# Layer 1 of a four-layer megakernel: the turning of a row's probabilities moved one row of scores later, and layer 2's layernorm rows turned in other banks

## The chip, the cores and the metric

The kernel runs on one core of a Trainium2 chip. It is one program of some 40,500 instructions that computes four transformer-like layers in one launch. The metric is the device time of one execution in microseconds (us). The kernel before takes 2910.99 us, the median of three runs (2909.49 to 2912.12).

The engines are named as in the profile: PE is TensorE, PEld its weight loads, DVE is VectorE, ACT is ScalarE, POOL is GpSimd, SP is SyncE, which issues DMAs.

## The reference

The input is x of 4 sequences with 512 tokens of width 256, in float32. Each of the four layers does

```
xn = layernorm(x)
x  = x + attention_i(xn) + ffn_i(xn)
```

with another kind of attention and feed-forward in each. The change touches layer 1's attention, and the layernorm that ends layer 1. Layer 1's attention has 16 heads, and keys and values that come from one compressed vector of 64 per token:

```
q     = rmsnorm(x @ wq_a) @ wq_b          -> 16 heads of 128 (plain) + 64 (rotary)
ckv   = x @ wkv_a                         -> 64 (compressed) + 64 (rotary, one for all heads)
kv    = rmsnorm(ckv[:64]) @ wkv_b         -> 16 heads of 128 (keys) + 128 (values)
probs = softmax(causal(q @ k.T * 192**-0.5))
x    += (probs @ v) @ wo
```

Layer 1's feed-forward is the sum of a gated unit of width 1024 and of a product-key memory: each token picks 8 of 512 experts, whose rows are gathered from HBM.

## The kernel before, in words

Everything is in tiles of 128 partitions. x stays in SBUF as 16 tiles of 128 tokens; `xnT` holds the layernormed x with the width on the partitions. Matrix products are float32, so that one product of the program is two passes on PE; a turn (transpose) of a 128x128 block is a product with the identity in one pass.

PSUM has eight banks, which `Ctx.ps` (L49) gives out under three tags: four "mm", two "tr" and two "acc". A bank is given out again once its last reader is done.

Layer 1's attention is `latent_pieces` (L1071). The heads' key and value weights are folded into the queries and the output weights (`carry`, L1095, once for each group of four heads), so that scores are taken against the compressed vector and its rotary part, `kf`, 128 rows in all, and the probabilities multiply the compressed values `cv`. After the projections, one loop (L1293) goes over 64 rows of scores: for each group of four heads, each sequence, each pair of heads, and each head of the pair. A row `s` is one head of one sequence, 512 queries by 512 keys, in four steps i = 0 to 3:

- `probabilities(s, i)` (L1153) calls `exp_scores` (L1035): PE takes the scores of query tile i against the first (i + 1) x 128 keys into an "mm" bank (L1042); DVE adds the mask, takes the extreme of each query and writes to SBUF (L1045); ACT takes the exponential and its sum (L1049). At i = 2 the sums of tiles 0 to 2, and at i = 3 that of tile 3, are inverted on DVE (L1165), and ACT scales the tiles by them (L1167).
- `turned(s - 1, i)` (L1169) turns, for the row before, the blocks of key tile j = i: 4 - j blocks (L1174) into a "tr" bank. The bank is copied to `PT` by DVE for j = 0 and 2 and by ACT for j = 1 and 3 (L1178); the copy is issued after the next step's turns.
- At i = 0 of odd rows the rotary part of the next queries is combined (`rotate`, L1146), and at i = 0 of even rows the next pair's queries are computed (`queries`, L1120, four wide products, copied out by ACT at L1137 to L1142).
- At the end of each even row, with both heads of the pair before turned, the product of values and probabilities (L1328, 16 narrow products in an "acc" bank) is taken; ACT copies it to `zT` (L1334), and `out_pieces` (L1275) multiplies it by the output weights (L1282) in pieces that later steps place between their own work.

These pieces are generators. `weave` (L566) draws from several of them by planned costs (each `yield` states one): the attention, the product-key memory (`product_key_pieces`, L1341, with gathers on POOL at L1435 and much work on DVE), the gated unit (`glu_pieces`, L224), and near the end the routing of layer 2's first half. The recording order is then not the final order: a scheduler places each engine's instructions by priority (the recording order) and by when it takes their inputs and banks to be ready, so that the order on each engine is its own. After that each engine runs its list strictly in order and waits on semaphores.

When all three contributions to a sequence of x are in, `layernorms` (L124) is called for it (L2339): DVE computes the statistics and the rows (L149), and after eight more steps PE turns them by 128x128 blocks, four to a bank, two banks to a sequence (L159), and ACT copies each bank into `xnT` (L164). The bank's tag is "mm" where `apart` is set and "tr" elsewhere.

## Time and profile before

| what | us |
|---|---|
| median of three runs | 2910.99 |
| the profiled execution, its own time | 2915.69 |
| its span, first to last instruction | 2913.9 |
| PE busy in the span | 2860.2 (98%) |
| PEld busy | 1920.8 (66%) |
| DVE busy | 2131.7 (73%) |
| ACT busy | 1401.9 (48%) |
| POOL busy | 862.4 (30%) |
| turns of probabilities in layer 1 (L1174) | 640 blocks, 857.2 to 1456.7 |
| mean granted TensorE clock | 0.996 |

The page's span is that of the profiled execution, which is an ordinary one with its own time; durations and waits come from it. A busy PE is drawn with modelled ends: products overlap in the pipeline, so that a product of 512 columns is drawn 0.59 long while the next may start 0.43 after it. A wait in the lists is the drawn idle time of an engine before an instruction, put down to what released it last. The granted clock is the share of full speed that TensorE ran at.

### The profile page before, as it was taken

What the parts mean: (1) busy time and instruction counts of PE and PEld (TensorE: products, weight loads), DVE (VectorE), ACT (ScalarE), POOL (GpSimd) and SP (SyncE); (2) the same over time, 40 slices, a digit from 0 to 9 for tenths busy, and PEclk for the clock granted to TensorE, in tenths of its full rate; (3) what the DMA queues carried; (4) which work ended last, traced back from release to release, by engine and by line L of the source; (5) the groups of instructions that cost most, each with busy time, mean ns of one, the idle gap of its engine ahead of it and who ended that gap; (6) DMA issues with size and microseconds to landing.
All of it is one profiled execution on the core that took longest, in us unless ns stands there. A gap on an engine that the chain in (4) does not pass through costs nothing.

```text
span 2913.9 us, 40511 instructions
## 1 busy us (share of the span) xinstructions
PE 2860.2 (98%) x13767; PEld 1920.8 (66%) x13767; DVE 2131.7 (73%) x5421; ACT 1401.9 (48%) x3354; POOL 862.4 (30%) x687
## 2 busy tenths in 40 slices
PE   9999999999999999999999999999999999999999
PEld 5566665666655655555577688888888756666666
DVE  6778778787778787888775687777777666666666
ACT  4444445454366666667733554444444333333332
POOL 0565655656510033333035100000000043333331
PEclk9999999999999999999999999999999999999999
DMA  2433333333320144444234544444444300000000
GB/s 106 119 109 115 113 98 95 109 116 97 109 82 17 54 101 124 116 107 112 79 120 120 164 118 125 144 130 130 147 124 141 102 1 22 22 22 22 22 1 30
DMA packets 138687, 268.60 MB, mean 92 GB/s; under 512 B 19729, under 2 KB 99105, under 8 KB 134129
## 3 DMA queue, kind: packets, MB, share of 16 engines
q1 hardware_dynamic: 124016, 218.20, 24.4%
q0 software_dynamic: 14176, 47.04, 6.5%
q8 instruction: 109, 1.79, 0.3%
q14 instruction: 98, 0.79, 0.1%
q10 hardware_dynamic: 288, 0.79, 0.1%
HBM read 202.25 MB, written 54.26 MB: 88 GB/s over the span
## 4 chain that ended last, share of the span: by engine, by line
PE 59%; DVE 7%; ACT 4%; DMA 2%; issue 1%; SPq 0%; POOL 0%; DVEq 0%; ACTq 0%
PE mm L358 17%; PE acc L358 7%; PE mm L1042 6%; PE tr L358 6%; PE acc L1709 5%; PE acc L1058 4%; PE mm L177 3%; PE acc L266 1%; PE acc L1328 1%; DVE pr L1045 1%; PE tr L1174 1%; ACT pr L1049 1%; PE mm L185 1%; PE mm L2121 1%; ACT pr L1167 1%
## 5 line engine op out<-in xcount | busy, mean ns | idle before, releaser
L1049 ACT ACTIVATE pr<-pr,nm 128x128 f32<-128x128 f32 (+3 forms) x512 | 286.4, 560 | 297.6 <-DVE nm L1045 293.4
L1045 DVE CUSTOM_DVE_ANT_0 pr<-mm,late 128x128 f32<-128x128 f32 (+3 forms) x512 | 246.0, 483 | 115.9 <-PE mm L1042 114.3
L177 PE MATMUL mm<-xnT,wu 128*128 128x512 f32 x624 | 283.2, 595 | 0.9 <-DVE cy L620 0.5
L369 ACT COPY part<-mm 128x512 f32<-128x512 f32 (+1 forms) x372 | 177.9, 479 | 210.8 <-PE mm L358 202.6
L358 PE MATMUL mm<-token_sums,unit_sums 128*128 128x512 f32 (+1 forms) x624 | 268.1, 512 | 3.6 <-ACT part L369 3.6
L1435 POOL DMA_INDIRECT e<-in_p_experts,ids x128 | 127.7, 998 | 463.7 <-DVE x L206 358.3
L177 PE MATMUL mm<-xnT,w_in 128*128 128x512 f32 x512 | 230.9, 594 | 2.8 <-DVE cy L620 2.8
L520 DVE SCALAR_TENSOR_TENSOR x<-acc,cw,x 128x128 f32<-128x128 f32 x372 | 128.7, 346 | 106.8 <-PE acc L358 105.1
L177 PEld LDWEIGHTS mm<-xnT,wu 128*128 128x128 f32 x624 | 115.4, 190 | 126.6 <-issue 117.9
L620 DVE SCALAR_TENSOR_TENSOR cy<-mm,ws,cy 128x509 f32<-128x509 f32 (+2 forms) x216 | 159.8, 744 | 40.9 <-ACT cy L616 37.1
L1042 PE MATMUL mm<-kf,qf 128*128 128x128 f32 (+3 forms) x512 | 180.2, 443 | 3.8 <-DVE nm L1045 1.9
L785 ACT ACTIVATE xD<-xc,ws 128x128 f32<-128x128 f32 x256 | 83.6, 390 | 193.3 <-POOL y L826 182.8
L802 POOL TENSOR_TENSOR G<-G,CB 128x1024 f32<-128x1024 f32 x64 | 151.1, 2361 | 76.8 <-DVE G L765 76.8
L1042 PE MATMUL mm<-k,q 128*128 128x128 f32 (+3 forms) x512 | 170.5, 438 | 2.6 <-DVE nm L1045 2.3
L358 PEld LDWEIGHTS acc<-down_sums,hidden_sums 128*128 128x128 f32 x744 | 111.7, 191 | 85.1 <-issue 83.4
L177 PEld LDWEIGHTS mm<-xnT,w_in 128*128 128x128 f32 x512 | 95.8, 190 | 107.2 <-issue 91.8
L1709 PEld LDWEIGHTS acc<-PT,V 128*128 128x128 f32 x1280 | 153.8, 193 | 5.1 <-issue 1.7
L1709 PE MATMUL acc<-PT,V 128*128 128x128 f32 x1280 | 153.9, 276 | 0.0
L302 POOL TENSOR_TENSOR down_sums<-wu 128x256 f32<-128x256 f32 x8 | 5.8, 730 | 498.4 <-DMA wu<-in_o_units 498.4
L765 DVE TENSOR_TENSOR_SCAN G<-G,eye 128x1024 f32<-128x1024 f32 x64 | 147.2, 2300 | 0.1
L1174 PEld LDWEIGHTS tr<-con,pr 128*128 128x128 f32 x640 | 82.3, 141 | 89.9 <-ACT pr L1167 26.7
L503 DVE TENSOR_TENSOR whole<-mm,part 128x512 f32<-128x512 f32 x128 | 88.5, 692 | 68.9 <-PE mm L358 68.9
(456 smaller groups left out, 6735.1 us busy)
## 6 DMA issues: line engine op xcount, KB each, us to landing
turned<-Y SPq DMA_DIRECT2D x252, 160.0 KB, 2.6
PT<-turned SPq DMA_DIRECT2D x63, 640.0 KB, 3.9
G<-own SPq DMA_DIRECT2D x64, 512.0 KB, 4.7
w_in<-in_m_units SPq DMA_DIRECT2D x16, 1024.0 KB, 5.9
eb<-since SPq DMA_DIRECT2D x96, 128.0 KB, 3.5
wu<-in_o_units SPq DMA_DIRECT2D x6, 1536.0 KB, 6.6
wo<-in_m_units SPq DMA_DIRECT2D x16, 512.0 KB, 4.3
psw<-pes SPq DMA_DIRECT2D x128, 64.0 KB, 2.0
```

Source lines behind the costliest of these rows:

```text
L177: c.nc.tensor.matmul(out, lhsT=w[:, d, cols], rhs=c.xnT[:, d, tokens], start=(d == 0), stop=(d == 1))
L358: self.kept(self.c.nc.tensor.matmul(bank, lhsT=lhsT, rhs=rhs, start=first, stop=True, skip_group_check=not first))
L369: self.c.nc.scalar.copy(r, bank)
L520: c.nc.vector.scalar_tensor_tensor(x, bank, self.factor(u, tt), x, ALU.mult, ALU.add)
L620: nc.vector.scalar_tensor_tensor(y[:, j:], src[:, : SEQ - j], conv[:, k, 3 - j : 4 - j], y[:, j:], ALU.mult, ALU.add,)
L765: tc.keep_in_program_order(nc.vector.tensor_tensor_scan(flat, flat, eye.rearrange("p h t -> p (h t)"), 0.0, ALU.mult, ALU.add))
L802: nc.gpsimd.tensor_mul(G, G, seqs[b][2][:, t, :][:, None, :].to_broadcast([P, HG, P]))
L1042: kept(nc.tensor.matmul(sc, lhsT=q[:, i * P : n], rhs=k[:, :n], start=True, stop=True))
L1045: nc.vector.tensor_tensor_reduce(out=pr, in0=sc, in1=late[:, SEQ - n :], scale=scale, scalar=-NEG, op0=ALU.add, op1=ALU.min, accum_out=nm,)
L1049: nc.scalar.activation(pr, pr, AF.Exp, bias=nm, scale=-1.0, accum_out=total)
L1435: nc.gpsimd.indirect_dma_start(out=e, out_offset=None, in_=a["p_experts"], in_offset=bass.IndirectOffsetOnAxis(ap=ids[:, t, k : k + 1], ax ...
L1709: kept(nc.tensor.matmul(zs[:, i], lhsT=head["V"][:, j, h, :], rhs=head["PT"][:, :, i * (i + 1) // 2 + j, :], start=(j == 0), stop=(j == i),))
```

## The change

Two edits. In the loop of layer 1 the four steps of 64 rows become one counter n, with s, i = divmod(n, 4); `turned` is called for step n - 5 instead of n - 4, which is one step of scores later, and the values' product follows the last turn of its pair, so that it too stands one step later, after the first step of the next row of scores. The placing of `rotate`, of `queries`, and of the pieces stays by i and s. The second edit gives `layernorm` and `layernorms` an argument `bank`, and the call for the layernorm after layer 1 passes "mm". From L1291 on, lines of the changed kernel have a number lower by one, and from L2339 on higher by one.

```
-def layernorms(c, seqs, lag, tokens=None, stats=None, apart=False):
+def layernorms(c, seqs, lag, tokens=None, stats=None, apart=False, bank="tr"):
...
-            pt = c.ps("mm" if apart else "tr")
+            pt = c.ps("mm" if apart else bank)
...
-    for s in range(65):
+    for n in range(4 * 65 + 1):
+        s, i = divmod(n, TPB)
         if s < 64:
-            prs[s] = []
-        for i in range(TPB):
-            if s < 64:
-                probabilities(s, i)
-            if s > 0:
-                if i == 0:
-                    PTs[s - 1] = c.tile(pool, [P, 1280], "PT")
-                ready, copy = copy, turned(s - 1, i)
-                if ready:
-                    ready()
-            if i == 0 and s % 2 == 1 and s < 63:
-                rotate(*turning)
-            yield 0.85
-            if i % 2:
-                yield from islice(pieces, 1)
-            if i == 0 and s % 2 == 0 and s < 62:
-                turning = queries(s // 2 + 1)
-                yield 2.6
-        if copy:
-            copy()
-            copy = None
-        if s > 0:
-            del prs[s - 1]
-        if s % 2 == 1:
-            continue
-        if s == 0:
+            if i == 0:
+                prs[s] = []
+            probabilities(s, i)
+        done, j = divmod(n - TPB - 1, TPB)
+        if done >= 0:
+            if j == 0:
+                PTs[done] = c.tile(pool, [P, 1280], "PT")
+            ready, copy = copy, turned(done, j)
+            if ready:
+                ready()
+        if i == 0 and s % 2 == 1 and s < 63:
+            rotate(*turning)
+        yield 0.85
+        if i % 2:
+            yield from islice(pieces, 1)
+        if i == 0 and s % 2 == 0 and s < 62:
+            turning = queries(s // 2 + 1)
+            yield 2.6
+        if done < 0 or j < TPB - 1:
+            continue
+        copy()
+        copy = None
+        del prs[done]
+        if done % 2 == 0:
             continue
...
-        p = s // 2 - 1
+        p = done // 2
...
-                    rhs=PTs[s - 2 + h][:, START[j] : START[j] + SEQ - j * P],
+                    rhs=PTs[done - 1 + h][:, START[j] : START[j] + SEQ - j * P],
...
-        c.parts(3, lambda b: layernorm(c, b, halves[b // 2][b % 2 * SEQ : (b % 2 + 1) * SEQ, :]))
+        c.parts(3, lambda b: layernorm(
+            c, b, halves[b // 2][b % 2 * SEQ : (b % 2 + 1) * SEQ, :], bank="mm"
+        ))
```

More of the change, by code (lines that the diff above doesn't have):

```diff
@@ L116, in rsqrt, with layernorm @@
     c.nc.vector.reciprocal(out, s)
-def layernorm(c, b, tokens=None, apart=False):
-    layernorms(c, [b], 8, tokens, apart=apart)
-def layernorms(c, seqs, lag, tokens=None, stats=None, apart=False):
+def layernorm(c, b, tokens=None, apart=False, bank="tr"):
+    layernorms(c, [b], 8, tokens, apart=apart, bank=bank)
+def layernorms(c, seqs, lag, tokens=None, stats=None, apart=False, bank="tr"):
     nc, pool = c.nc, c.ln
```

## The prediction

> **What bounds the kernel now.** I read the busy time by stage first, then who waits on TensorE in the stage that the change touches, then single waits in the timeline. The stage of layer 1's rows of scores runs from 857 to 1462 us. Columns: stretch, its length, busy time and instructions of PE, PEld, DVE, ACT and POOL, granted clock, DMA share, GB/s.

> ```profile
> 0.00:857.00 857.00, 842.42 (x3939) 521.20 (x3939) 658.48 (x987) 397.84 (x858) 440.41 (x299) 1.00 0.35 106
> 857.00:1462.00 605.00, 587.77 (x2728) 343.69 (x2728) 486.96 (x1694) 411.25 (x1091) 120.81 (x122) 0.99 0.33 88
> 1462.00:2914.00 1452.00, 1429.96 (x7103) 1055.94 (x7101) 986.23 (x2742) 592.83 (x1406) 301.17 (x266) 1.00 0.29 86
> ```

> TensorE is the bound in all three, and in the stage it is drawn idle for 605.0 - 587.8 = 17.2 us, the most per microsecond of the three. Only time that TensorE loses there can come back. The same stage's waits (us in total, times, longest), first of the matmuls, then of the weight loads:

> ```profile
> PE tr L1174 <- ACT pr L1167: 5.3, 14, 1.5
> PE tr L1174 <- ACT PT L1178: 3.5, 4, 1.4
> PE mm L1042 <- DVE nm L1045: 1.9, 2, 1.1
> PE tr L1174 <- DVE PT L1178: 1.4, 5, 0.5
> PE tr L159 <- ACT PT L1178: 1.2, 1, 1.2
> ```
> ```profile
> PEld tr L1174 <- ACT pr L1167: 26.7, 67, 2.0
> ...
> PEld tr L1174 <- ACT PT L1178: 12.6, 20, 2.0
> PEld tr L1174 <- DVE PT L1178: 9.3, 18, 1.0
> ```

> The turned probabilities (L1174) wait most: for the scaled probabilities (L1167), and for one of the two "tr" banks to be emptied (L1178). The first list is too small and the second too large, as one wait shows:

> ```profile
> 1262.20 0.49 PE L1174 MATMUL tr<-con,pr 128*128 128x128 f32 x3
> 1262.92 0.33 PE L1174 MATMUL tr<-con,pr 128*128 128x128 f32 x1 [0.23 <-ACT pr L1167]
> ```

> Turned blocks that wait for nothing start 0.109 us apart (median of the trace), so the fourth was due at 1262.20 + 3 x 0.109 = 1262.53 and came at 1262.92: 0.39 us lost, where the view draws 0.23, since a last block is drawn 0.273 long. I took the starts of all matmuls of the stage in this way, with the median distances 0.109, 0.215, 0.322 and 0.429 us for 128, 256, 384 and 512 columns. Lost before L1174: 13.3 us to L1167, 8.2 us to L1178, 3.4 us with no releaser. Lost before L1042: 7.5 us to other engines (5.0 of them to L1045). Lost before L159: 2.7 us. These are the prices below.

> Two waits cost clock as well (timeline, then windows around them):

> ```profile
> 1130.68 0.87 PE L1174 MATMUL tr<-con,pr 128*128 128x128 f32 x2 [1.50 <-ACT pr L1167]
> ```
> ```profile
> 1444.40 0.77 PE L159 MATMUL tr<-con,xn 128*128 128x128 f32 x4 [1.18 <-ACT PT L1178]
> ...
> 1446.98 1.11 PE L159 MATMUL tr<-con,xn 128*128 128x128 f32 x4
> ```
> ```profile
> 1126.00:1139.00 13.00, 11.23 (x47) 6.93 (x47) 8.25 (x24) 5.58 (x15) 5.89 (x7) 0.74 0.56 144
> ...
> 1441.00:1449.00 8.00, 5.84 (x17) 2.48 (x19) 7.92 (x26) 7.37 (x18) 0.00 (x0) 0.79 0.21 68
> ```

> The granted clock was 0.74 over 13 us and 0.79 over 8 us: 13 x 0.26 = 3.4 us and 8 x 0.21 = 1.7 us of TensorE time are lost. The trace records the clock at 0.5 for 6.8 us from 1130.8 and for 3.4 us from 1444.8.

> **The change part by part.** No instruction is added or removed: in the built programs each engine has the same kinds and counts. POOL's order is the same; on SP only one DMA of the routing moves, past the four swaps of one query; layers 0, 2 and 3 keep their orders, apart from the bank of eight groups at L159. So everything happens between 857 and about 1475 us. Within it the orders do move, so the change does what it says.

> (a) *Turned blocks later.* I laid the built orders of both programs out in TensorE time by the distances above, and took for each of the 640 blocks the distance from the end of its own score to its turn. Median before 6.57 us, after 8.24; nearer than 5 us before 167, after 82. In the trace, from the end of a score to the end of its scaling takes at the median 3.87 us for the last row of four (from 3.40 up; upper quarter 4.46) and 4.12 for the third. Near blocks are thus the ones at risk, and the 167 near ones carry 8.1 of the 13.3 us, 0.049 each. At that price 82 carry 4.0: a gain of 4.1. The 473 farther ones carry 5.1 us because ScalarE or VectorE was late; distance does not cure that, and I leave it. Ends: all 13.3 gone; or a loss of 1.5, if the far ones, now 558, keep their price by distance and the near ones lose nothing. I take -4.1.

> (b) *The two "tr" banks.* A bank is free when its copy (L1178) ends: at the median 1.85 us after the turn for the first copy of a row (VectorE) and 1.29 for the second (ScalarE; upper quarter 2.13). The bank of the first is wanted by the third after 1.40 us of TensorE work before, 1.83 after; that of the second by the fourth after 1.72 before, 1.29 after. One gains what the other loses: 0. Ends: -8.2, all that is lost today, and +8.2, the same again.

> (c) *The values' product one row later.* Its wait for VectorE's copy has 2.68 us of TensorE work before it now and 5.6 after; it loses 0.2 us today. 0. The wait for ScalarE's copy has 2.04 in both. What is queued behind it, the next score, moves with it.

> (d) *Banks of the scores.* L1042 waits on L1045 in 86 places before and 53 after. It waits on the copy of the rotary queries (L1137) in 26 places instead of 11, mostly 1.84 us of work or more after the products; that copy ends 0.82 us after them at the median, 1.73 at the ninth tenth. So cover stays: 0, between -7.5 (all that L1042 loses) and +5 (its loss to L1045 again).

> (e) *Layernorm rows in "mm".* At 1444.40 the rows of one sequence waited 1.18 us drawn, 1.34 by starts, for a "tr" bank that a copy of probabilities held, and at 1446.98 another 0.48 for their own first copy. With four banks neither is in the way, and the built order turns both halves block by block between two scores. What is late next is the rows themselves (L149, four in 1.38 us), and a score stands behind them. I take 1.8 of waits and 0.7 of the 1.7 us of clock: -2.5; ends -4.4 and +3 (two such waits and no clock back).

> (f) *Clock at 1130.8.* It goes if the wait at 1130.68 goes. That wait stands among the products that prepare a group's weights, with the copy queue behind a late VectorE; the chance is even: -1.7, ends -3.4 and +3.4 (one more such stretch).

> Sum: 4.1 + 2.5 + 1.7 = 8.3 us less. The profiled execution took 2915.7 us (span 2913.9 and 1.8 around it), 4.7 more than the median of 2911.0: 2915.7 - 8.3 - 4.7 = **2902.7**.

> [...]

> **The rivals.** *The wait only moves* (about 2909): VectorE is busy 487.0 of 605.0 us (80%) and ScalarE 411.3 (68%); if TensorE waits since they are behind, time won at L1174 is lost at the next score's bank. For it: 5.1 of 13.3 us are lost at far blocks, and VectorE releases L1042. Against: both engines idle for over 100 us. Then (a) and (f) are nothing and the 1.8 us of (e) stay.

> *Slower, by the second "tr" bank* (about 2919): half of ScalarE's copies end later than the 1.29 us that are left. If they still do, the upper half, 32 of 64 rows, pays some 0.4 us (half of 2.13 - 1.29), 13 us; at 1.72 the upper quarter, 16 rows, pays about 0.4, 6.5. That is +6.5, and one more half-clock stretch, +1.7: 8.2 over the median. It decides where ScalarE's median copy ends past 1.29 us. Against: blocks come to ScalarE's queue more evenly.

> *All waits go* (about 2890): 13.3 + 4.4 + 3.4 = 21.1 less, if far blocks were late only because near ones bunched ScalarE's work.

> **How the numbers follow.** Forecast (4 to 14 us less) 0.45, the wait moves 0.25, all go 0.16, slower 0.14. A measurement here tells some 0.2% (5.8 us) from no change. Faster by more: 0.16 and nearly nine tenths of the forecast, 0.55. Within: the rest of it, 0.06, and nine tenths of the moved wait, 0.29. Slower: 0.16. The range for 8 in 10 leaves half of the slower case out above and the end of the fast one below: 2890 to 2916; the forecast's own is 2897 to 2907.

> **What would show it.** Right: weight loads before L1174 wait under 20 us on L1167 instead of 26.7; L159 no longer waits on L1178; the stage from first to last turned block is some 8 us shorter, and the rest as long. Wrong: PE's waits on L1178 (4.9 us drawn) doubled, a new wait of L1042 on L1045 or on L164, L159 on L149 over 1 us, or a further stretch at half clock.

## The result, and the profile after

The changed kernel takes 2920.4 us (median of 6 runs, 2915.8 to 2923.2), the kernel before beside it 2911.4 (6 runs, 2906.9 to 2917.5): a ratio of 1.0027 with the interval [1.0016, 1.0038]. It is slower by about 9 us. Run once more beside the kernel before it was 2917.7 (12 runs) against 2911.3 (31 runs), 1.0022 [1.0014, 1.0031], which is 6 us. The prediction said 2902.7 and 2890 to 2916. (What the title calls one row of scores is one step i, a quarter of a row `s`.)

About half of the loss is clock. Every run has its granted clock on record, to 0.001: the mean is 0.9960 over those 12 runs and 0.9972 over the 31, and 0.0012 x 2914 = 3.5 us is what that costs TensorE. At an equal clock the kernels are closer: 2917.7 against 2915.5 in the median at 0.996 (8 and 5 runs), 2914.6 against 2911.3 at 0.997 (2 and 15). That the longer waits below bring the lower clock fits the last section, and was not tried apart from them.

The profiled execution of the changed kernel took 2921.1 us, its span 2919.3. Stages of it, cut at the same events as before (first turned block; 5 us past the last); columns as before:

```profile
0.00:860.00 860.00, 845.09 (x3939) 523.33 (x3939) 658.94 (x985) 397.63 (x858) 440.37 (x299) 1.00 0.34 106
860.00:1468.00 608.00, 585.38 (x2728) 346.91 (x2728) 485.56 (x1695) 414.72 (x1091) 119.50 (x122) 0.99 0.34 87
1468.00:2919.30 1451.30, 1430.08 (x7103) 1055.91 (x7101) 987.61 (x2742) 592.04 (x1406) 300.86 (x266) 1.00 0.29 86
```

Only the middle stage can be the change's own work, and there TensorE is drawn idle for 608.0 - 585.4 = 22.6 us instead of 17.2. The same stage's waits of the matmuls, and then of the weight loads ahead of turned blocks and of the values' product (L1327 is L1328 of the kernel before):

```profile
PE tr L1174 <- ACT PT L1178: 7.0, 7, 1.9
PE tr L1174 <- DVE PT L1178: 5.3, 7, 1.3
PE acc L1327 <- DVE PT L1178: 3.8, 3, 2.0
PE mm L159 <- DVE xn L149: 3.3, 2, 2.2
PE tr L1174 <- ACT pr L1167: 1.3, 5, 0.5
```
```profile
PEld tr L1174 <- DVE PT L1178: 17.8, 24, 2.1
PEld tr L1174 <- ACT PT L1178: 12.9, 14, 2.6
PEld tr L1174 <- ACT pr L1167: 7.0, 21, 0.8
PEld acc L1327 <- DVE PT L1178: 5.7, 5, 2.5
```

The wait that the change was to end has all but ended: on L1167 the weight loads wait 7.0 us instead of 26.7, the matmuls 1.3 instead of 5.3. In its place stand the copies of turned blocks (L1178): 12.3 us on the matmuls at L1174 instead of 4.9, and 3.8 at the values' product, which waited 0.2 before.

Why the copies are late is read on VectorE. Its waits (us in total, times, longest) on the rotary product of the next pair's queries, which needs four transfers of swapped rows (L1139), first in the kernel before, then in the changed one:

```profile
DVE psw L1149 <- DMA psw<-pes: 16.8, 13, 3.1
```
```profile
DVE psw L1149 <- DMA psw<-pes: 26.2, 14, 3.4
```

One such wait in the changed kernel's timeline, VectorE and then TensorE:

```profile
1229.91 0.08 DVE L1045 DVE_READ_ACCUMULATOR2_ANT nm<- 128x1 f32 x1
1232.24 0.69 DVE L1149 TENSOR_TENSOR psw<-psw,tab 128x512 f32<-128x512 f32 x1 [2.25 <-DMA psw<-pes]
1232.85 0.68 DVE L1045 CUSTOM_DVE_ANT_0 pr<-mm,late 128x512 f32<-128x512 f32 x1
...
1233.55 0.26 DVE L1045 CUSTOM_DVE_ANT_0 pr<-mm,late 128x128 f32<-128x128 f32 x1
...
1233.73 0.42 DVE L1178 COPY PT<-tr 128x256 f32<-128x256 f32 x1
```
```profile
1230.41 0.38 PE L1174 MATMUL tr<-con,pr 128*128 128x128 f32 x2
...
1231.06 2.15 PE L1327 MATMUL acc<-PT,cv 128*64 128x512 f32 x10
1234.21 0.86 PE L1327 MATMUL acc<-PT,cv 128*64 128x256 f32 x6 [1.00 <-DVE PT L1178]
```

The third key tile's two blocks are turned at 1230.41 to 1230.79 and could be copied at once: VectorE idles for 2.25 us. But the head of its queue is the rotary product, whose rows have not landed, and behind it stand two reductions of scores; the copy starts at 1233.73 and the values' product, which reads it, stops for 1.00 us. In the kernel before the same copy stands ahead of the same rotary product, and the same values' product does not stop:

```profile
1233.28 0.42 DVE L1178 COPY PT<-tr 128x256 f32<-128x256 f32 x1
1233.94 0.69 DVE L1149 TENSOR_TENSOR psw<-psw,tab 128x512 f32<-128x512 f32 x1 [0.24 <-issue]
```
```profile
1233.88 2.37 PE L1328 MATMUL acc<-PT,cv 128*64 128x512 f32 x16
```

What TensorE lost, by the starts of matmuls as in the prediction (each wait over 0.04 us), between the first score of layer 1 and the first turned rows of layer 2's experts, in us; for the values' product it is the time of the 32 products above the shortest, 2.30 each. Each loop has two profiles here, since single ones differ by 2 to 4 us in the sum: e2 has the loop of the kernel before, e0 is the changed kernel again. e15 and e16, the old and the new loop with nothing waiting for the transfer, are told of below.

| lost at | before | e2 | changed | e0 | e15 (old) | e16 (new) |
|---|---|---|---|---|---|---|
| L1174, scaled probabilities | 13.2 | 13.1 | 3.5 | 3.4 | 9.8 | 2.8 |
| L1174, copies | 8.2 | 9.4 | 15.5 | 13.9 | 5.6 | 9.4 |
| values' product | 3.4 | 6.0 | 12.0 | 11.4 | 3.4 | 7.4 |
| L159, layernorm rows | 1.8 | 1.8 | 4.0 | 4.0 | 2.8 | 2.9 |
| sum | 26.6 | 30.3 | 35.0 | 32.7 | 21.6 | 22.5 |

The means of the two loops are 28.5 and 33.9 us: +5.4, most of the 6 to 9 that were measured. The row of the values' product is a time, so it also holds what these products lost at half clock: 1.7 us in e2, 2.3 in changed, 2.0 in e0, 2.8 in e16, and 0.1 or less in the other two. Without that the means are 27.6 and 31.7, +4.1.

### The profile page after: what moved, and what is told of

It reads as the page before. It is cut to its first block, busy times and chain, and to the rows that moved or that the text cites. A ratio compares the mean times of both kernels' runs of the same rounds, so it can differ in the third digit from the quotient of the medians.

```text
span 2919.3 us, 40515 instructions
## 1 busy us (share of the span) xinstructions
PE 2860.5 (98%) x13767; PEld 1926.1 (66%) x13767; DVE 2132.1 (73%) x5421; ACT 1404.4 (48%) x3354; POOL 860.7 (29%) x687
## 4 chain that ended last, share of the span: by engine, by line
PE 61%; DVE 5%; ACT 3%; DMA 2%; issue 1%; SPq 1%; POOL 0%; DVEq 0%; ACTq 0%
PE mm L358 17%; PE mm L1042 7%; PE acc L358 7%; PE tr L358 6%; PE acc L1708 5%; PE acc L1058 4%; PE mm L177 3%; PE acc L1327 2%; PE acc L266 2%; PE tr L1174 2%; DMA psw<-pes 1%; PE acc L1282 1%; PE mm L185 1%; PE mm L2120 1%; ACT pr L1049 1%
## 5 line engine op out<-in xcount | busy, mean ns | idle before, releaser
L1045 DVE CUSTOM_DVE_ANT_0 pr<-mm,late 128x128 f32<-128x128 f32 (+3 forms) x512 | 244.9, 481 | 111.2 <-PE mm L1042 109.8
L1042 PE MATMUL mm<-kf,qf 128*128 128x128 f32 (+3 forms) x512 | 181.9, 443 | 1.5 <-DVE qf L1151 0.6
L1042 PE MATMUL mm<-k,q 128*128 128x128 f32 (+3 forms) x512 | 170.2, 437 | 2.5 <-DVE nm L1045 1.9
L1174 PEld LDWEIGHTS tr<-con,pr 128*128 128x128 f32 x640 | 82.1, 141 | 80.2 <-issue 23.3
```

The source lines that it names most:

```text
L1042: kept(nc.tensor.matmul(sc, lhsT=q[:, i * P : n], rhs=k[:, :n], start=True, stop=True))
L1045: nc.vector.tensor_tensor_reduce(out=pr, in0=sc, in1=late[:, SEQ - n :], scale=scale, scalar=-NEG, op0=ALU.add, op1=ALU.min, accum_out=nm,)
L1174: nc.tensor.transpose(pt[:, (i - j) * P : (i - j + 1) * P], prs[s][i][:, j * P : (j + 1) * P], c.ident)
```

## The experiments

Every run stands beside runs of the kernel before on the same chip, 2909.8 to 2911.5 us in the median; behind its time stand the ratio to these and its 95% interval. "Theory A": the loop's edit is good for the waits on scaled probabilities, and the rotary product's wait for its transfer, which stands in front of the copies, spoils it.

**The halves of the change.** e0 is the changed kernel again, e1 has the loop's edit alone, e2 the layernorm's bank alone, and e3 calls `rotate` a step later:

```
e1:  c, b, halves[...], bank="tr"     (for "mm"; the loop as changed)
e2:  the kernel before, with bank="mm" in that call
e3:  -        if i == 0 and s % 2 == 1 and s < 63:
     +        if i == 1 and s % 2 == 1 and s < 63:
              rotate(*turning)
```

> The changed kernel itself, as the yardstick for the others on the same chip. Both theories: 7 to 10 us over the kernel before (2918 to 2921 where that has 2911).

> The changed kernel with the layernorm rows back in the "tr" banks: the loop's edit alone. Theory A (the loop's edit only moves the wait: the copies of turned banks stand late in VectorE's and ScalarE's queues, behind the rotary product that waits for its DMA; the loop then gives no gain, and some loss): 2 to 6 us over before. Theory B (the loop's edit gains, the layernorm rows in "mm" cost it all, since TensorE then waits in order for VectorE's rows at L159, 3.3 us drawn, and for a copied bank, and loses clock after it): 0 to 5 us under before, and 8 to 12 under the changed kernel.

> The kernel before with the layernorm rows in the "mm" banks: the second edit alone. Theory A: within 3 us of before. Theory B: 5 to 10 us over before, with 2 to 4 us of drawn waits of L159 on L149.

> The changed kernel with the rotary combination (rotate) one step of scores later, at i = 1 of odd rows, so that its product on VectorE stands later in the queue and its DMA has one step more. Theory A: VectorE's wait for that DMA falls from 26 us to under 15 in the stage, TensorE's waits for copies of turned banks (12.3 us drawn before L1174 and 3.8 before the values' product) fall by a third or more, and the time by 3 to 8 us against the changed kernel. If the banks are late by their number alone (a rival, C), the DMA wait falls and the time stays within 3 us of the changed kernel.

Measured: e0 2917.7 us (1.0022 [1.0014, 1.0031]), e1 2918.1 (1.0020 [1.0012, 1.0029]), e2 2911.3 (0.9999 [0.9989, 1.0008]), e3 2919.4 (1.0025 [1.0015, 1.0036]). The loop's edit alone makes the loss, the bank of the layernorm rows makes none; theory B falls. e3 gained nothing, and its trace says why that is no verdict on A: VectorE still waits 19.7 us for the transfer, and in the built program the product stands behind the same score's reduction in nearly all pairs, wherever the loop calls it. What places it is the planner; that it reckons with a transfer that lands earlier than it does is a guess.

**Without the transfer.** e4 and e5, the changed kernel and the one before:

```
-        for to in range(0, P, 32):
-            nc.sync.dma_start(psw[to : to + 32, :], pes[to ^ 32 : (to ^ 32) + 32, :])
...
-        tc.keep_in_program_order(nc.vector.tensor_mul(psw, psw, sinq))
+        tc.keep_in_program_order(nc.vector.tensor_mul(psw, pes, sinq))
```

> The changed kernel without the four transfers that bring the swapped rows of a pair's queries (L1139): the rotary product reads pes in place of psw, so the rotation leaves out the swap of rows. VectorE then never waits for a transfer ahead of that product (26.2 us of waits in the changed kernel). Theory A (the loop edit is good for TensorE's waits on scaled probabilities, and what spoils it is the rotary product's wait for its transfer, which stands on VectorE directly ahead of the next copies out of the turned banks and of the next row's scores): the waits of L1174 and L1327 on copies (16.1 us drawn on PE between 857 and 1475) fall under 8, and the time falls to 2903 to 2910, at or under the same probe of the kernel before. Rival C (two turned banks and the copies' own places are too tight, whatever the product waits for): the time stays 6 us or more above the same probe of the kernel before, and the waits on copies stay above 12.

> The kernel before with the same part left out (no swap of rows in the rotation, no transfer, the product reads pes): the control. Theory A: the product's wait of 16.8 us there stood ahead of nothing that TensorE wanted soon, so the time moves little, 2906 to 2912. Rival C says the same of this one; what tells the two apart is the distance between this and the changed kernel with the same part left out: A says the changed one is 2 to 8 us faster than this, C that it is 6 or more slower.

Measured: e4 2898.4 us (0.9958 [0.9945, 0.9970]), e5 2897.2 (0.9948 [0.9935, 0.9961]). The distance between the two loops falls from 6 to 9 us to 1.2, with overlapping intervals. So the loss hangs on the transfer; rival C, that the turned banks alone make it, falls. But A missed twice. The changed loop is not 2 to 8 us faster than the old one here, and the kernel before, whose wait I had called harmless, gains 14 us.

**Held later, and a third bank.** e6 queues the product on VectorE behind the odd row's third reduction; e7 turns the fourth block in a general bank:

```
e6:  -        tc.keep_in_program_order(nc.vector.tensor_mul(psw, psw, sinq))
     +        with tc.issue_after(c.reduced.ins):      (the last reduction of L1045)
     +            tc.keep_in_program_order(nc.vector.tensor_mul(psw, psw, sinq))
     -        if i == 0 and s % 2 == 1 and s < 63:
     +        if i == 2 and s % 2 == 1 and s < 63:
e7:  -        pt = c.ps("tr")
     +        pt = c.ps("tr" if j < 3 else "mm")
```

> The changed kernel, all of its work done, with the rotary product queued on VectorE behind the reduction of the third score of its odd row (in the changed kernel it stands behind the first, whatever the place of the call in the loop). The transfer has some 4 us more to land, and the copies and reductions of the first two steps go ahead of the product. Theory A: VectorE's wait for the transfer falls from 26.2 to under 10 us, the waits of L1327 on VectorE's copy (3.8 drawn) go, those of L1174 on copies (12.3) fall by half or more, and the time falls to 2905 to 2913; the price is a later qf, whose reader is two steps off: under 2 us of new waits of L1042 on L1150 or L1151. Rival C: the waits on copies stay, and the time with them, at 2916 to 2921.

> The changed kernel with the fourth turned block of each row (one transposition, copied by ScalarE) in one of the four general banks, so that three blocks a row share the two turned banks. Rival C (the number of turned banks is the limit): the waits of L1174 on copies fall from 12.3 us drawn on PE to under 6, and the time falls by 4 to 9 us, to 2909 to 2914. Theory A: the copies come as late as before; a bank more hides a part of it: the waits of L1327 on the copy of the third block (3.8) stay, the time falls by 0 to 4 us, to 2914 to 2919.

Measured: e6 2927.9 us (1.0053 [1.0040, 1.0066]), e7 2917.3 (1.0018 [1.0009, 1.0026]). In e6 VectorE's wait for the transfer is gone from the list, and the copies' waits are 7.7 drawn instead of 12.3, as A said. The price was mis-sized: qf is late for the next row's first score, and its probabilities with it (matmuls, between 840 and 1475 us; the lines' numbers are one higher here):

```profile
PE tr L1175 <- ACT pr L1168: 15.7, 16, 2.4
...
PE mm L1042 <- DVE qf L1152: 3.9, 4, 2.0
```

e7's time is where A had it, 1 us or so under the changed kernel, and not where C had it, though the values' product waits 0.8 drawn instead of the 3.8 that A left it: TensorE still loses 11.2 us there by the starts, 3.4 of them at half clock, against 12.0 and 11.4. (Its profile is of an execution of 2910.9 us, 6 under its median.) The number of banks is at most a small part.

**The transfer two scores earlier.** e8 (on the kernel before) and e9 (on the changed one) issue the products, `pes` and the transfers at the third score of the odd row; e11 and e12 also hold both rotary products at the place that they had, e12 with copies at once (e10, below):

```
+        return p, pes, psw, pl
+
+    def halves(p, pes, psw, pl):
         qf = c.tile(pool, [P, 2, SEQ], "qf")
...
+        if i == 2 and s % 2 == 1 and s < 61:
+            coming = queries(s // 2 + 2)
+            yield 2.0
         if i == 0 and s % 2 == 0 and s < 62:
-            turning = queries(s // 2 + 1)
-            yield 2.6
+            turning = halves(*(coming if s else queries(1)))
+            yield 0.6
```

> The kernel before, all of its work done, with the two products of a pair's queries, the copy to pes and the four transfers put two scores earlier (at the third score of the odd row, in place of the first of the next even row); the copies out of the other product into qf stay where they are, so qf needs no third buffer, and one general bank is held two scores longer. The transfer has some 4 us more to land, and the rotary product keeps its place on VectorE. The probes without the transfer took 14 us off the kernel before (2911.1 to 2897.2) and 20 off the changed one (2918 to 2898.4). Theory A (the product's wait for the transfer delays the scores and copies that are queued behind it on VectorE): the wait of 16.8 us falls under 6, and the time falls to 2898 to 2906. Rival D (the probes gained by what they left out, SyncE's queue and 8 MB of transfers that meet the gathers and weights, and not by the wait): the wait falls, the time stays within 3 us of 2911.

> The changed kernel with the same: products, pes and transfers two scores earlier. Theory A: VectorE's wait of 26.2 us for the transfer falls under 8, the time falls from 2918 to 2899 to 2907, within 3 us of the same edit on the kernel before, since the two probes without the transfer were 1.2 us apart. Rival D: 2915 to 2921.

> The kernel before with transfers two scores earlier, as in the run of that name, and both rotary products (with cosq and with sinq) held on VectorE behind the reduction of the odd row's first score, where the second stands in the kernel before: the earlier run's own new wait (18.6 us of the product with cosq for ScalarE's copy pes, since it had moved ahead) is taken out. Theory A (the wait is what costs): VectorE's waits at the two products fall under 3 us together, and the time from 2911 to 2898 to 2906, near the probe without the transfer (2897). Rival D (the transfers' work is what costs): the waits fall, the time stays at 2907 to 2914.

> The changed kernel with the same, and each block's copy issued right after its transpositions. Theory A together with E (the transfer's wait and the copies' late place are two causes): 2895 to 2903, at or under e11. Theory A alone (copies at once gained only because they slipped ahead of the wait): about 2898 to 2906, as e11. Rival D: 2908 to 2914, as with copies at once alone (2911.9).

Measured: e8 2916.1 us (1.0021 [1.0012, 1.0030]), e9 2920.6 (1.0035 [1.0021, 1.0048]), e11 2917.5 (1.0021 [1.0012, 1.0030]), e12 2917.4 (1.0020 [1.0012, 1.0029]). Theory A missed in all four; of D's ranges only e9's held, and there the wait had not gone: the product with cosq waited 22.3 us for ScalarE instead. In e8 one wait took another's place: the planner had moved the product with cosq ahead, where it waits for ScalarE's copy (VectorE, 840 to 1475 us; numbers three higher):

```profile
DVE pec L1151 <- ACT pes L1137: 18.6, 13, 5.4
...
DVE psw L1152 <- DMA psw<-pes: 10.9, 6, 5.1
```

e11 took that out too and left 3.1 us of the wait, and was no faster. Its TensorE lost 10.9 us to scaled probabilities instead of 13.1, and more in many small places: against e2, whose loop is the same, 2.2 us before scores, 1.8 without a releaser before turns, 2.7 before products outside these groups. Which part of the edit (a general bank held longer, TensorE's order, or ScalarE's) makes these is open. By these four alone theory D, that the transfers' work costs and not the wait, could not be ruled out.

**Wait or work.** e15 and e16 keep the transfers and let nothing wait for them:

```
-        tc.keep_in_program_order(nc.vector.tensor_mul(psw, psw, sinq))
-        nc.vector.tensor_add(qf[:KL, 1, :], pec[:KL, :], psw[:KL, :])
-        nc.vector.tensor_add(qf[KL:, 0, :], pec[KL:, :], psw[KL:, :])
+        tc.keep_in_program_order(nc.vector.tensor_mul(pec, pec, sinq))
+        nc.vector.tensor_add(qf[:KL, 1, :], pec[:KL, :], pes[:KL, :])
+        nc.vector.tensor_add(qf[KL:, 0, :], pec[KL:, :], pes[KL:, :])
```

> The kernel before with the four transfers into psw kept, and nothing reading them: in place of the product of psw with sinq stands one of the same shape on pec, and the two sums take pes in place of psw, so the rotation leaves out the swap. The transfers' work is all there, VectorE's wait of 16.8 us for them is not. Theory A (the wait costs): 2895 to 2901, as without the transfers (2897.2). Rival D (the work costs): 2907 to 2913.

> The changed kernel with the same: transfers kept, nothing waits for them. Theory A: 2896 to 2902, as without the transfers (2898.4), and the time that TensorE loses at the values' product falls by 6 us or more, as it did there. Rival D: 2914 to 2920.

Measured: e15 2900.3 us (0.9964 [0.9950, 0.9977]), e16 2901.6 (0.9965 [0.9953, 0.9977]). D falls. The wait, with the late place that goes with it, costs the kernel before 2911.5 - 2900.3 = 11 us and the changed one about 2918 - 2901.6 = 16; the transfers' own work is at most the 3 us between these and e4 and e5, whose intervals overlap with theirs. Both add up. Ahead of the stage the first pair's rotation waits for nothing either: the first score came at 839.4 and 842.2 us, where the two profiles of each loop have 844.2 and 847.3 in the mean, 4.8 and 5.1 less; 0.9 and 1.7 of that is half clock in layer 0, near 786 us, which some executions of either loop have and some do not. Within the stage the table's sums fall from 28.5 to 21.6 in the old loop, 6.9, and from 33.9 to 22.5 in the new one, 11.4. So the same wait costs the new loop some 4.5 us more than the old, by single profiles without it, and what is left between the two without it, 0.9 by the table and 1.4 by the times, is within 0.2%. But for the clock the new loop might even be ahead there: its runs have 0.9963 in the mean against e15's 0.9972, and e4 0.9972 against e5's 0.9986, which is worth some 2.5 and 4 us where the times differ by 1.4 and 1.2. These are five or six runs each. In some pairs the built product stands a few scores earlier than it did, so these probes take out the wait and the late place that goes with it, not the one without the other. The matmuls' waits of e16 between 840 and 1475 us:

```profile
PE tr L1174 <- ACT PT L1178: 4.1, 5, 1.9
PE tr L1174 <- DVE PT L1178: 2.4, 5, 1.2
...
PE tr L1174 <- ACT pr L1167: 1.1, 3, 0.7
...
PE acc L1327 <- DVE PT L1178: 0.4, 1, 0.4
```

The values' product waits 0.4 instead of 3.8, and the copies 6.5 instead of 12.3. The 6.5 are still more than e15's 2.5:

```profile
PE tr L1174 <- ACT pr L1167: 3.7, 8, 1.6
...
PE tr L1174 <- ACT PT L1178: 1.3, 3, 0.5
...
PE tr L1174 <- DVE PT L1178: 1.2, 4, 0.5
```

**Copies at once.** e10 (changed kernel), e14 (kernel before) and e13 (changed, without the transfers) issue each block's copy with its turn:

```
-            ready, copy = copy, turned(done, j)
-            if ready:
-                ready()
+            turned(done, j)()
...
-        copy()
-        copy = None
```

> The changed kernel with each turned block's copy issued right after the block's own transpositions and not a step later, so that it stands on VectorE and ScalarE ahead of the next score's reduction and exponential. Asked is what held the banks: if the copies' own place behind the next score's reduction is what matters (rival E), TensorE's waits on copies (12.3 us drawn at L1174, 3.8 at L1327) fall by half and the time falls by 4 to 9 us, to 2909 to 2914. Theory A: the wait for the transfer still stands ahead of copies and scores, the wait of 26.2 us stays above 20, and the time stays at 2914 to 2921.

> The kernel before with each block's copy issued right after its transpositions, the control for that edit. If the copies' late place is a fault that only the changed order has (theory E as stated: the third block's copy falls behind the next row's first score and ahead of the values' product), the time stays within 3 us of 2911. If early copies are good in any order, it falls by 4 to 8 us as in the changed kernel, to 2903 to 2907.

> The changed kernel without the swap's four transfers (the product reads pes; the rotation leaves out the swap of rows) and with each block's copy issued at once. If the two causes are separate (A with E), the prediction's gain shows here: 2889 to 2895, 2 to 8 us under the kernel before without the transfers (2897.2). If the waits of the turned blocks cannot be bought off (rival F: what the scaled probabilities gain, the copies lose, whatever their place), it stays at 2896 to 2900.

> A version: the kernel before with each block's copy issued right after its transpositions (2904.7 alone), and layer 2's layernorm rows turned in the general banks (the change's second part, 2911.3 alone against 2911.3). If the two add as measured: 2903 to 2906. The copies-at-once kernel shows 2.1 us of waiting of those rows for a copy out of a turned bank, which this takes away, against new waits for the rows themselves of 1 to 2 us: 2902 to 2907.

Measured: e10 2911.9 us (1.0004 [0.9995, 1.0013]), e14 2904.7 (0.9975 [0.9965, 0.9984]), e13 2898.2 (0.9953 [0.9940, 0.9966]), e17 2905.5 (0.9982 [0.9973, 0.9991]). Early copies are worth 5 to 6 us in either order (some 2.6 of e14's are clock, 0.9981 in the mean against 0.9972), so their late place was no fault of the changed loop alone, and e14 is the version that beats both kernels; the layernorm rows add nothing to it. In e14's built program the third block's copy stands ahead of the fourth score's reduction in 59 of 64 rows, where the kernel before has 39. The first copy of a row now ends 0.93 us after its turn at the median and 1.61 at the upper tenth, where the kernel before has 1.20 and 2.62. Its matmuls' waits (840 to 1475 us):

```profile
PE tr L1174 <- DVE PT L1178: 4.0, 6, 1.5
PE tr L1174 <- ACT pr L1167: 3.7, 13, 0.7
...
PE tr L1174 <- ACT PT L1178: 0.8, 2, 0.6
```

Without the transfers early copies gave the changed loop nothing (2898.2 against 2898.4). That is where rival F had the time. In the trace one wait takes the other's place: against e4 the copies wait 3.3 us drawn instead of 7.0, the scaled probabilities 3.4 instead of 1.1.

## Why the prediction was wrong

The mechanism of (a) was right, and its cover was not free: steps (b) and (c), each set at 0, took back more than (a) gave, some 5 us of it by a wait that I had not looked at; and (e) and (f), which counted on 0.7 + 1.7 = 2.4 us of clock back, met some 3.5 us of clock lost. By its steps:

- **(a) turned blocks later, -4.1.** Right in kind and too small: 13.2 to 3.5, 9.7 us less. The far blocks, which I left at their price, gained as well.
- **(b) the two "tr" banks, 0.** Failed: 8.8 to 14.7 in the mean of two profiles, +5.9, towards the end of +8.2 that I had written down. I weighed only how long TensorE works between a bank's use and its reuse, and held the copies where they were. They moved: the first copy of a row ended 1.85 us after its turn at the upper quarter before and 2.85 after, 2.62 and 4.25 at the upper tenth, with the rotary product in front of it. A third of it is that wait: in e16 against e15 the rise is 3.8. A slip of reading too: the 1.85 and 1.29 us that the text calls medians are the upper quarters of that trace; the medians are 1.20 and 0.75, and the 2.13 is the upper tenth.
- **(c) the values' product later, 0.** Failed: 4.7 to 11.7, +7.0, of which 1.3 is half clock. The "0.2 us today" was the drawn wait alone; by its time the product lost 3.4 already. My cover of 5.6 us for VectorE's copy counted TensorE's work and not VectorE's queue, where the copy now stood behind a product that idles for a transfer and behind the next row's first reduction. Without the wait the rise is 4.0, and 2.8 of that is half clock.
- **(d) banks of the scores, 0.** Right. L1042 waits 0.2 us drawn on the rotary copy and 0.6 on L164, and no longer shows L1045.
- **(e) layernorm rows, -2.5.** Its two halves cancel: the wait for a copy's bank went, and "what is late next is the rows themselves" came true, 3.3 us drawn at L159 on L149. Alone it is 0.9999 of the kernel before; in the changed loop e0 and e1 are 0.4 us apart.
- **(f) clock at 1130.8, -1.7.** The stretch is absent after, and absent in e2 too, whose loop is the old one and has nearly the same wait there (1.36 us drawn at 1126.96). That one stretch was chance of one run. But the term's sign failed too: over many runs the change lowers the granted clock from 0.9972 to 0.9960, 3.5 us lost where 1.7 were to come back. The two profiles hide that, since the one of before is an execution at 0.996. In the changed profile waits of 1.86 us at 1409.81 and 2.22 us at 1446.56 were followed by new stretches; between first score and layer 2 both profiles have 13.7 us at half clock.

With (d) at 0 and L159's 2.2 the measured steps add to -9.7 + 5.9 + 7.0 + 2.2 = +5.4, or +4.1 without the half clock in (c). The starting point was right too: the 4.7 us that the profiled execution stood over the median were taken off, and the kernel before stayed at 2911.

Of the rivals, "slower, by the second 'tr' bank" had sign and size, 2919, by a cause that was not the one at work: ScalarE's copies, whose median it wanted past 1.29 us, ended at 0.52 at the median, upper quarter 1.41. The copies that came late were VectorE's, and the reason stood one instruction ahead of them. "The wait only moves" is what is left when the transfer's wait is taken out: from e15 to e16 the scaled probabilities give 7.0 us, and the copies and the values' product take 7.8, 2.8 of them at half clock. The sign that I named for wrong, PE's waits on L1178 doubled, is what the profile showed, with 12.3 for 4.9, and so did L159 on L149 over 1 us. Two signs for right came as well, 7.0 us for 26.7 on L1167 and no L159 on L1178; the third did not: from the first turned block to the last it is 602.4 us for 599.5.

The view that would have told it was in the profile before: VectorE's list of waits had 16.8 us on the rotary product in this stage. I put each edit's cover in TensorE's time, and never asked what stands at the head of VectorE's queue at the new place of the copies and of their reader.

## What to carry to other kernels

Cover counted in the bound engine's time was worth nothing where the instruction that fills it sat behind another's wait (5.6 us of it here, and the values' product lost 11.7 us instead of 4.7): for every moved producer and consumer, read what is ahead of it in its own engine's queue, above all an instruction that waits for a transfer. A call moved in the source need not move an instruction that a planner places, as e3 shows; read its place in the built order, and hold it there if the place matters. And where copies release scarce banks, issue them ahead of the next reduction: here that edit alone was worth 6 us.

## What the runs showed of the hardware

**The transfer lands later in the second part of the stage, in some profiles.** The four transfers of 64 KB each take 2.0 us at the median from issue to landing up to 1148 us and 3.4 from there to 1462, where the expert rows' gathers double, in the kernel before (issues, KB each, median us to landing; first stretch, then second):

```profile
psw<-pes SPq DMA_DIRECT2D x60, 64.0 KB, 2.0
e<-in_p_experts,ids POOLq DMA_INDIRECT x40, 4.3
```
```profile
psw<-pes SPq DMA_DIRECT2D x60, 64.0 KB, 3.4
e<-in_p_experts,ids POOLq DMA_INDIRECT x80, 4.8
```

That fits where the loss is: in the changed profile the first 32 rows of scores take 7.6 us less than in the kernel before (3.4 of them its clock at 1130.8), and the rest of the stage 10.3 more (3.4 of them further half clock). VectorE's wait for the transfer is 8.4 us up to 1150 and 17.8 from there to 1470, where the kernel before has 7.7 and 9.1. The gathers' number alone is not the reason for the slower landing: with the same gathers (75 to 80 of them in the second stretch) the median is 2.7 us in the changed kernel, 2.6 in e16 and 2.0 in e15. What else makes it is open.
